# State-space stage of a decoder: products, scores and counts put in other places of the turns

## The chip, the cores and the metric

The kernel runs on one core of one Trainium2 chip. The metric is the device time of one execution in microseconds; of a kernel that was run several times, the median is given. A core has five engines with a queue of instructions each: TensorE (PE in the profile; PEld is its loading of weights), VectorE (DVE), ScalarE (ACT), GpSimd (POOL) and SyncE (SP, here the queue that issues transfers). Engines wait for one another by semaphores; within its queue each takes the instructions in order.

## The reference

The whole is a decoder of two layers on 2048 tokens of width 256 (16 blocks of 128). Each of its parts is `x = layernorm(x + part(x))`. The change touches one of them alone, the state-space part of the second layer, with a small memory behind it:

```python
xn = rmsnorm(x); zxbcdt = xn @ in_proj_w              # z 512, xBC 768, dt 8
xBC = silu(conv_b + four taps along the tokens of xBC)  # 128 tokens in a sequence
y = ssd(xs * dt, dt * A, B, C) + xs * D               # 8 heads of 64, state 128, chunks of 64
y = rmsnorm(y * silu(z)) @ out_proj_w
scores = sigmoid(relu(y @ scorer_w1) @ scorer_w2)      # one for each token
summaries = y @ summ_w                                 # 64 wide
# a scan over all tokens keeps the 50 summaries of the highest scores over 0.5
q = y @ q_w; kk = pool @ k_w; vv = pool @ v_w
retrieved = softmax(q kk / 4, valid slots) @ vv
y = y + sigmoid([y, retrieved] @ gate_w) * retrieved   # if the scores' mean is over 0.3
return x + y
```

The kernel replaces the scan by ranks: for each token it counts how many scores are larger (or equal, and of an earlier token). A token with a rank under 50 and a score over 0.5 goes into that slot of the pool.

## The kernel before

Six stages follow one another; this one is `stage3`, which calls `ssm` (lines 1246 to 1768) and then `memory` (line 1771). Stage 4, cross attention, follows.

**Blocks, groups and turns.** A block is 128 tokens, a group four blocks (512 tokens). `squared`, `normed` and `turn` normalise and transpose the four groups ahead of the loop; group 0 is convolved there too. Then a loop of 18 turns runs (line 1683), n from 0 to 17. In `ssm` every engine takes its instructions in the order in which they are written; no planner reorders them there. (In `memory` only TensorE's order is as written, the other engines' is planned.) Turn n carries several blocks at once, each at another step:

- block n + 1: `decay` (line 1388, GpSimd, cs less csb into mT, two mT buffers), `inner` (1399: TensorE products of B and C, and transposes; VectorE reads them as bc and xd), `decayed` (1394, ScalarE twice), `joined` (1412, GpSimd, mT times bc)
- block n: `outer` (1441, TensorE, needs mT and xd), `skipped` (1451, VectorE, four instructions), `passed` (1459, GpSimd: yf times the gate sz)
- block n - 1: `measured` (1463, ScalarE squares yf into sq), `added` (1469, GpSimd, two adds that bring the four chunks of sq down to one), `projected` (1475, TensorE), `summed` (1481: one TensorE product with a column of ones, then ys on VectorE and the root yrs on GpSimd), `scaled` (1490: y on ScalarE, x on VectorE)
- block n - 2: `kept` (1496: TensorE transposes y, ScalarE copies it into yT)
- block n + 2: `spread` (a transfer of csb, on SyncE's queue; two csb buffers) and `gate`, `gate_tanh`, `gated` (1417 to 1439)
- two chunks of the next group's convolution: `convolved`, `taps`, `tanh`, `curved` (1290 to 1316), in turns with n % 4 < 3 and n < 11. So turns 3, 7 and 11 to 15 carry no convolution.

In turns with n % 4 < 3 `inner`, `decayed` and `joined` stand early in the turn, in the others behind `summed`. PSUM has 8 banks: four ps_m, two ps_o (projected sums, transposed y, summaries, key and value banks), one ps_y (outer, and every third key or value bank) and one ps_s, which `inner`, `summed`, scores and keys take one after the other.

**Scores and ranks.** Once a group's four blocks are in yT, `remembered(g)` (1503) makes in one go the hidden layer and the queries (TensorE L1507, VectorE, ScalarE), the summaries (L1515) and the scores (L1519, then ScalarE and VectorE). It runs at the end of turns 7, 11 and 13 and, for group 3, after the loop. `lined` and `ranked` (1529, 1537) spread the group's scores along a row and keep them as keys. `counted(g)` (1551) gives three functions: `equals` (VectorE, three instructions), `by_vector(b)` (VectorE, one or two instructions that compare the row with a key and sum up) and `by_scalar(b)` (the same with signs on ScalarE, and a small correction on GpSimd). The table `counts` (1678) says in which turn which block's counts are made; group 3's follow after the loop, half on each engine.

**Between them** `others(n)` (1605) works off key and value banks of stage 4: TensorE products, a ScalarE copy, a store on SyncE's queue. There are twelve.

**After the loop** `memory` runs twelve key and value parts of stage 4 on TensorE first (line 1791; two PSUM banks, each copied out by ScalarE, rows L1998, L2001, L2018 and L2022), while VectorE sums up ranks and makes the picks (L1795 to L1808); then TensorE gathers the pool (L1810), and so on.

Of the kernel before, what the change touches and what calls it, by code (L numbers as in the profile page):

```python
# [1245 lines left out]
def ssm(K, w, m, kv_banks):  # L1246
# [6 lines left out]
    with ExitStack() as ctx:  # L1253
# [16 lines left out]
        def normed(g):  # L1270
            rs = K.new(small, [P, 4], F32, "rs")
            K.rsqrt(small, rs, xn[g].ss, 1.0 / D, 1e-5, "rs_t")
            t = K.new(work, [P, SH, P], F32, "csb").rearrange("p (i h) t -> p i (h t)", i=4)
            xn[g].x = [t[:, i, :] for i in range(4)]
            for i in range(4):
                nc.vector.tensor_scalar(xn[g].x[i], x[4 * g + i], rs[:, i:i + 1], None, ALU.mult)
# [181 lines left out]

        def passed(n):
            s, at = st[n], slice(n % 2 * P, n % 2 * P + P)  # L1460
            nc.gpsimd.tensor_tensor(s.yf, s.yf, sz[n // 2][:, :, at], ALU.mult)
# [19 lines left out]
        def summed(n):  # L1481
            s = st[n]
            pn = K.new(ps, [P, 1], F32, "ps_s", bufs=1)
            nc.tensor.matmul(pn, s.sq[:, 0, :], K.ones[:, :1], start=True, stop=True)
# [18 lines left out]
        def remembered(g):  # L1503
# [4 lines left out]
            hid = K.new(work, [P, 512], F32, "acc", bufs=3)  # L1508
# [7 lines left out]
            nc.vector.tensor_copy(m.summ[:, 4 * g:4 * g + 4, :], psu)  # L1516
            psc = K.new(ps, [P, 4], F32, "ps_s", bufs=1)
# [133 lines left out]
        for n in range(2):  # L1651
# [27 lines left out]
            11: ((equals0, None), (vector0, 0, 1, 2, 3)), 13: ((equals1, None), (vector1, 4, 5), (scalar1, 0, 1)),  # L1679
            14: ((vector1, 6, 7), (scalar1, 2, 3)), 15: ((equals2, None), (vector2, 8, 9), (scalar2, 0, 1, 2, 3)),  # L1680
            16: ((vector2, 10, 11), (scalar2, 4, 5, 6, 7)),
        }
        for n in range(NB + 2):
# [10 lines left out]
            if old:  # L1694
                measured(n - 1)
                added(n - 1)
# [9 lines left out]
            if new and i < 3:  # L1706
                inner(n + 1)
            if late is not None:
                curved(*late)
            if new and i < 3:  # L1710
                decayed(n + 1)
                joined(n + 1)
            if n in (8, 12, 14):
                lined({8: 0, 12: 1, 14: 2}[n])
# [13 lines left out]
            if new and i == 3:  # L1728
# [3 lines left out]
            if n in (12, 14, 15):  # L1732
                others(1)
            if n == NB:
                others(2)
# [6 lines left out]
            if 1 < n <= NB + 1:  # L1742
# [8 lines left out]
            if n in (7, 11, 13):  # L1751
                remembered({7: 0, 11: 1, 13: 2}[n])
# [5 lines left out]
            if n in (8, 12, 14):  # L1758
                ranked({8: 0, 12: 1, 14: 2}[n])
        remembered(3)  # L1760
        lined(3)
        ranked(3)
        equals, by_vector, by_scalar = counted(3)
        equals(None)
        for k in range(8):
            by_scalar((0, 1, 2, 3, 4, 5, 14, 15)[k])
            by_vector((6, 7, 8, 9, 10, 11, 12, 13)[k])
# [855 lines left out]
```

## Time and profile before

| | us |
|---|---|
| median of 3 runs | 1404.76 (1403.98 to 1405.64) |
| the profiled execution, its own time | 1408.86 |
| its span, first to last instruction | 1407.2 |
| mean granted TensorE clock | 0.954 |
| busy in the span: PE, DVE, ACT, POOL | 1234.8, 824.7, 676.4, 495.5 |
| loop of turns and the scores after it (first square at 415.3, last keys at 656.2) | 240.9 |

Busy time is a mean over stages with different limits: TensorE is 88% busy over the whole, but in this stage it is not what the others wait for. A timeline row reads: start, length, engine, line of the kernel, operation, what it writes and reads with shapes, how many instructions are merged in the row, and in brackets how long the engine sat idle before and what ended that. TensorE's fp32 products show as two records each. Three rows of turn 7 as samples: the sum over sq behind the halving adds, then the gate product of block 7 and the decay of block 9 behind it on GpSimd.

```profile
530.92 0.38 PE L1484 MATMUL ps_s<-ones,sq 128*128 128x1 f32 x2 [1.41 <-POOL sq L1472]
```

```profile
535.32 1.26 POOL L1461 TENSOR_TENSOR yf<-yf,sz 128x512 f32<-128x512 f32 x1 [0.45 <-DVE yf L1455]
536.54 1.90 POOL L1390 TENSOR_TENSOR mT<-cs,csb 128x1024 f32<-128x1024 f32 x1
```

### The profile page before, as it was taken

The numbers are of one execution on the slowest core, as the hardware profiler recorded it, in microseconds if no ns is written. First come the engines' busy times: TensorE is split into PE (matmuls) and PEld (weight loads), VectorE is DVE, ScalarE is ACT, GpSimd is POOL, SyncE is SP. The second block draws the span as 40 slices with busy tenths as digits, with TensorE's granted clock in tenths as the row PEclk, the third lists the DMA queues.
The fourth block names the chain that finished last, engine by engine and source line by source line (L and its number), as shares of the span: only waits on it lengthen the run. The fifth ranks groups of instructions, "written<-read, shape, count | busy, mean of one in ns | idle before, by whom it ended". The sixth has DMA issues, their size and how long they took to land.

```text
span 1407.2 us, 19229 instructions
## 1 busy us (share of the span) xinstructions
PE 1234.8 (88%) x6731; PEld 843.2 (60%) x6743; DVE 824.7 (59%) x1755; ACT 676.4 (48%) x1733; POOL 495.5 (35%) x669
## 2 busy tenths in 40 slices
PE   4678887889978899866998999999889999999995
PEld 1455444666654566643655788877777655666553
DVE  7799968989957887856244565667333111211115
ACT  5779865778956665544223566654522111111110
POOL 4256547668861776640043233222202000000003
PEclk9899989989999999987899999999999999999998
DMA  8358324110011211100100222211005222232002
GB/s 311 131 174 295 114 79 85 17 39 31 32 50 60 74 51 46 53 16 24 52 0 1 73 78 62 75 61 45 1 8 187 71 98 68 78 105 96 17 8 75
DMA packets 63120, 103.53 MB, mean 74 GB/s; under 512 B 11920, under 2 KB 41712, under 8 KB 62768
## 3 DMA queue, kind: packets, MB, share of 16 engines
q1 hardware_dynamic: 60848, 96.76, 20.6%
q0 software_dynamic: 2176, 5.55, 1.9%
q8 instruction: 53, 0.87, 0.3%
q14 instruction: 43, 0.35, 0.1%
HBM read 81.74 MB, written 16.35 MB: 70 GB/s over the span
## 4 chain that ended last, share of the span: by engine, by line
PE 52%; DVE 29%; ACT 8%; POOL 6%; issue 4%; DMA 1%; another core or an unknown queue 0%; SPq 0%; DVEq 0%; ACTq 0%; POOLq 0%
PE ps_y L2453 7%; PE ps_m L2442 7%; PE ps_g L2442 7%; PE ps_m L1998 4%; DVE acc L1306 2%; PE ps_m L2129 2%; ACT s L2100 2%; PE ps_t L2120 2%; PE ps_m L2018 2%; DVE cT L1315 1%; DVE s L915 1%; DVE m L2094 1%; DVE s L2090 1%; PE ps_t L2109 1%; PE ps_s L2087 1%
## 5 line engine op out<-in xcount | busy, mean ns | idle before, releaser
L82 POOL TENSOR_SCALAR ln_t<-ln_mv 128x1 f32<-128x1 f32 (+1 forms) x84 | 16.6, 197 | 450.7 <-DVE ln_mv L90 309.1
L2447 DVE TENSOR_TENSOR h<-h,ps_m 128x512 f32<-128x512 f32 x60 | 41.3, 688 | 228.3 <-PE ps_m L2442 228.3
L2100 ACT ACTIVATE s<-s,m 128x128 f32<-128x128 f32 x256 | 99.4, 390 | 69.1 <-DVE m L2094 69.1
L2446 ACT ACTIVATE h<-ps_g 128x512 f32<-128x512 f32 x60 | 35.8, 597 | 171.0 <-PE ps_g L2442 171.0
L2442 PE MATMUL ps_g<-xin,w 128*128 128x512 f32 x224 | 106.3, 592 | 0.0
L2442 PE MATMUL ps_m<-xin,w 128*128 128x512 f32 x224 | 105.3, 592 | 0.0
L2453 PE MATMUL ps_y<-w,h 128*128 128x256 f32 x448 | 97.8, 379 | 0.0
L2453 PEld LDWEIGHTS ps_y<-w,h 128*128 128x128 f32 x448 | 85.1, 190 | 14.6 <-issue 3.3
L2104 POOL TENSOR_TENSOR s<-s,t 128x1024 f32<-128x1024 f32 x32 | 60.7, 1898 | 90.7 <-DVE t L2103 90.7
L927 ACT ACTIVATE s<-s,m 128x128 f32<-128x128 f32 x256 | 83.3, 395 | 11.7 <-DVE m L922 11.7
L2442 PEld LDWEIGHTS ps_m<-xin,w 128*128 128x128 f32 x224 | 42.5, 190 | 51.4 <-issue 50.2
L2442 PEld LDWEIGHTS ps_g<-xin,w 128*128 128x128 f32 x224 | 42.0, 190 | 46.4 <-issue 45.0
L1998 PE MATMUL ps_m<-xT,half 128*128 128x256 f32 x256 | 62.6, 389 | 2.6 <-DVE qT L2003 1.9
L2454 ACT COPY y<-ps_y 128x256 f32<-128x256 f32 x30 | 11.2, 372 | 104.7 <-PE ps_y L2453 67.7
L2090 DVE TENSOR_TENSOR s<-ps_s,hide 128x1024 f32<-128x1024 f32 x32 | 39.2, 1224 | 35.9 <-PE ps_s L2087 35.9
L2129 PE MATMUL ps_m<-half,oT 128*128 128x256 f32 x256 | 59.3, 385 | 0.0
L1306 DVE SCALAR_TENSOR_TENSOR acc<-ps_m,l1a_conv_w,acc 128x508 f32<-128x508 f32 (+2 forms) x72 | 53.3, 740 | 3.5 <-ACT acc L1299 1.8
L1998 PEld LDWEIGHTS ps_m<-xT,half 128*128 128x128 f32 x256 | 47.4, 194 | 9.2 <-DVE qT L2003 2.3
L2129 PEld LDWEIGHTS ps_m<-half,oT 128*128 128x128 f32 x256 | 47.4, 190 | 7.5
L83 POOL TENSOR_TENSOR ln_rs<-ln_t,mhalf 128x1 f32<-128x1 f32 (+1 forms) x84 | 48.7, 579 | 7.0
L2100 ACT ACTIVATION_READ_ACCUMULATOR s<-s,m 128x1 f32 x256 | 48.2, 188 | 0.0
L1414 POOL TENSOR_TENSOR mT<-mT,bc 128x1024 f32<-128x1024 f32 x16 | 37.8, 2360 | 28.4 <-ACT mT L1396 16.3
(524 smaller groups left out, 3102.1 us busy)
## 6 DMA issues: line engine op xcount, KB each, us to landing
w<-in_w_gate_dram SPq DMA_DIRECT2D x9, 1024.0 KB
csb<-cs_dram SPq DMA_DIRECT2D x16, 512.0 KB
w<-in_l1f_gateT_dram SPq DMA_DIRECT2D x14, 512.0 KB
w<-in_l1f_upT_dram SPq DMA_DIRECT2D x14, 512.0 KB
w<-in_l1f_downT_dram SPq DMA_DIRECT2D x14, 512.0 KB
k<-kv SPq DMA_DIRECT2D x20, 256.0 KB
v<-kv SPq DMA_DIRECT2D x20, 256.0 KB
ring<-k SPq DMA_DIRECT2D x10, 512.0 KB
```

Of the source, the lines that this page charges most:

```text
L83: return self.nc.gpsimd.tensor_tensor(out, t, self.mhalf[: out.shape[0], :n], ALU.pow)
L927: nc.scalar.activation(at, at, AF.Exp, bias=m[h][:, i:i + 1])
L1306: nc.vector.scalar_tensor_tensor(accv[:, :, j:], pcv[:, :, :P - j], w.conv[:, c, TAPS - 1 - j:TAPS - j], accv[:, :, j:], ALU.mult, ALU.add,)
L1414: nc.gpsimd.tensor_tensor(st[n].mT, st[n].mT, bc, ALU.mult)
L1998: nc.tensor.matmul(pq[:, j, :], wt[k][:, at], src[:, k, :], start=(k == 0), stop=(k == KD - 1))
L2090: nc.vector.tensor_tensor(half(b, j), pss.rearrange("p r c k -> p (r c) k"), hide.unsqueeze(1).to_broadcast([P, 8, P]), ALU.add,)
L2100: nc.scalar.activation(at, at, AF.Exp, bias=m[j][:, i:i + 1], accum_out=t[j][:, i:i + 1])
L2104: nc.gpsimd.tensor_tensor(half(b, j), half(b, j), t[j].unsqueeze(2).to_broadcast([P, 8, P]), ALU.mult)
L2129: nc.tensor.matmul(py[b], oT[b][:, c, :], w.o[c // 4][:, c % 4, :], start=(c == 0), stop=(c == NC - 1))
L2442: nc.tensor.matmul(ps[:, j, :], m[k][:, c * P:(c + 1) * P], self.r.xin[:, k, e, cols], start=(k == 0), stop=(k == KD - 1),)
L2447: nc.vector.tensor_tensor(h, h, pu, ALU.mult)
L2453: nc.tensor.matmul(pd, rows(c), w.down[c // 4][:, c % 4, :], start=(c == 0), stop=(c == FI // P - 1))
```

## The change

`full(n)` names the turns with convolution, n < 11 and n % 4 < 3. In the other turns the gate product `passed` goes to VectorE, `added` falls away (`summed` multiplies all four chunks of sq with the ones and sums in PSUM instead), and `inner`, `decayed`, `joined` stand behind `summed` in turns 12 to 14 too. `remembered` is cut in two: `hidden_scores`, ahead of `outer`, with hidden layer, queries and summaries, and `scored`, at the end of the turn, with the scores. Group 2 has both in turn 14 instead of 13, and its row and keys in turn 15 instead of 14. The counts are spread over turns 11 to 17 in another way; VectorE's counts of group 2 (blocks 8 to 11) move behind the loop, and there all counts of group 3 are VectorE's. `others` moves from turns 12, 14, 15 and twice 16 to 12, 13, 15, 16 and 17; in turn 16 `kept` comes ahead of it. Ahead of the loop, half of the products of `normed` go to GpSimd for groups 2 and 3.

```diff
@@ -1273,7 +1273,8 @@
             t = K.new(work, [P, SH, P], F32, "csb").rearrange("p (i h) t -> p i (h t)", i=4)
             xn[g].x = [t[:, i, :] for i in range(4)]
             for i in range(4):
-                nc.vector.tensor_scalar(xn[g].x[i], x[4 * g + i], rs[:, i:i + 1], None, ALU.mult)
+                on = nc.gpsimd if g > 1 and i > 1 else nc.vector
+                on.tensor_scalar(xn[g].x[i], x[4 * g + i], rs[:, i:i + 1], None, ALU.mult)

         def turn(g):
             xnT[g] = K.new(grp, [P, KD, 512], F32, "xnT", bufs=4)
@@ -1456,9 +1457,13 @@
                     s.yf[:, c, :], cT[n // 4][:, c, mine(n)], w.d[:, c:c + 1], s.py[:, c, :], ALU.mult, ALU.add,
                 )

+
+        def full(n):
+            return n < 11 and n % 4 < 3
+
         def passed(n):
             s, at = st[n], slice(n % 2 * P, n % 2 * P + P)
-            nc.gpsimd.tensor_tensor(s.yf, s.yf, sz[n // 2][:, :, at], ALU.mult)
+            (nc.gpsimd if full(n) else nc.vector).tensor_tensor(s.yf, s.yf, sz[n // 2][:, :, at], ALU.mult)

         def measured(n):
             s = st[n]
@@ -1481,7 +1486,9 @@
         def summed(n):
             s = st[n]
             pn = K.new(ps, [P, 1], F32, "ps_s", bufs=1)
-            nc.tensor.matmul(pn, s.sq[:, 0, :], K.ones[:, :1], start=True, stop=True)
+            chunks = 1 if full(n + 1) else DI // P
+            for c in range(chunks):
+                nc.tensor.matmul(pn, s.sq[:, c, :], K.ones[:, :1], start=(c == 0), stop=(c == chunks - 1))
             t = K.new(small, [P, 1], F32, "ys")
             nc.vector.tensor_scalar(t, pn, 0.25 / DI, 1e-5, ALU.mult, ALU.add)
             s.yrs = K.new(small, [P, 1], F32, "yrs")
@@ -1500,12 +1507,12 @@
             nc.scalar.copy(m.yT[:, :, n * P:(n + 1) * P], pt)


-        def remembered(g):
+        def hidden_scores(g):
             cols = slice(512 * g, 512 * g + 512)
             pq = K.new(ps, [P, 512], F32, "ps_m", bufs=4)
             for k in range(KD):
                 nc.tensor.matmul(pq, w.qw1[:, k, :], m.yT[:, k, cols], start=(k == 0), stop=(k == KD - 1))
-            hid = K.new(work, [P, 512], F32, "acc", bufs=3)
+            hid = held["hid"] = K.new(work, [P, 512], F32, "acc", bufs=3)
             nc.vector.tensor_scalar(hid[SUM:, :], pq[SUM:, :], 0.0, None, ALU.max)
             nc.scalar.copy(m.qT[:, cols], pq[:SUM, :])
             psu = K.new(ps, [P, 4, SUM], F32, "ps_o")
@@ -1514,6 +1521,9 @@
                 for k in range(KD):
                     nc.tensor.matmul(psu[:, i, :], m.yT[:, k, at], w.summ[:, k, :], start=(k == 0), stop=(k == KD - 1))
             nc.vector.tensor_copy(m.summ[:, 4 * g:4 * g + 4, :], psu)
+
+        def scored(g):
+            hid = held["hid"]
             psc = K.new(ps, [P, 4], F32, "ps_s", bufs=1)
             for i in range(4):
                 nc.tensor.matmul(
@@ -1676,9 +1686,9 @@
         order, late = (4, 5, 0, 1, 2, 3), None
         (equals0, vector0, _), (equals1, vector1, scalar1), (equals2, vector2, scalar2) = (counted(g) for g in range(3))
         counts = {
-            11: ((equals0, None), (vector0, 0, 1, 2, 3)), 13: ((equals1, None), (vector1, 4, 5), (scalar1, 0, 1)),
-            14: ((vector1, 6, 7), (scalar1, 2, 3)), 15: ((equals2, None), (vector2, 8, 9), (scalar2, 0, 1, 2, 3)),
-            16: ((vector2, 10, 11), (scalar2, 4, 5, 6, 7)),
+            11: ((equals0, None), (vector0, 0, 1)), 12: ((vector0, 2, 3),),
+            13: ((equals1, None), (vector1, 4), (scalar1, 0, 1)), 14: ((vector1, 5), (scalar1, 2, 3)),
+            15: ((vector1, 6, 7),), 16: ((equals2, None), (scalar2, 0, 1, 2, 3)), 17: ((scalar2, 4, 5, 6, 7),),
         }
         for n in range(NB + 2):
             g, i = divmod(n, 4)
@@ -1693,7 +1703,8 @@
                 gate_tanh()
             if old:
                 measured(n - 1)
-                added(n - 1)
+                if full(n):
+                    added(n - 1)
             if late is not None:
                 tanh(*late)
             if ahead:
@@ -1703,15 +1714,15 @@
                     gated()
                 gate(n + 2)
                 gate_tanh()
-            if new and i < 3:
+            if new and full(n):
                 inner(n + 1)
             if late is not None:
                 curved(*late)
-            if new and i < 3:
+            if new and full(n):
                 decayed(n + 1)
                 joined(n + 1)
-            if n in (8, 12, 14):
-                lined({8: 0, 12: 1, 14: 2}[n])
+            if n in (8, 12, 15):
+                lined({8: 0, 12: 1, 15: 2}[n])
             if ahead:
                 taps(*c[0])
                 tanh(*c[0])
@@ -1725,21 +1736,27 @@
                 curved(*c[0])
             if old:
                 summed(n - 1)
-            if new and i == 3:
+            if new and not full(n):
                 inner(n + 1)
                 decayed(n + 1)
                 joined(n + 1)
-            if n in (12, 14, 15):
+            if n in (7, 11, 14):
+                hidden_scores({7: 0, 11: 1, 14: 2}[n])
+            if n in (12, 13, 15):
                 others(1)
             if n == NB:
-                others(2)
+                kept(n - 2)
+                others(1)
             if now:
                 outer(n)
                 skipped(n)
                 passed(n)
             if old:
                 scaled(n - 1)
-            if 1 < n <= NB + 1:
+            if 1 < n < NB:
+                kept(n - 2)
+            if n > NB:
+                others(1)
                 kept(n - 2)
             if ahead:
                 taps(*c[1])
@@ -1748,23 +1765,26 @@
                     gate(n + 2)
             else:
                 late = None
-            if n in (7, 11, 13):
-                remembered({7: 0, 11: 1, 13: 2}[n])
+            if n in (7, 11, 14):
+                scored({7: 0, 11: 1, 14: 2}[n])
             if n == 13:
                 held["junk"] = K.new(work, [P, SH, P], F32, "csb").rearrange("p h t -> p (h t)").bitcast(BF16)
             for what, *which in counts.get(n, ()):
                 for b in which:
                     what(b)
-            if n in (8, 12, 14):
-                ranked({8: 0, 12: 1, 14: 2}[n])
-        remembered(3)
+            if n in (8, 12, 15):
+                ranked({8: 0, 12: 1, 15: 2}[n])
+        hidden_scores(3)
+        vector2(8)
+        scored(3)
         lined(3)
         ranked(3)
-        equals, by_vector, by_scalar = counted(3)
+        for b in (9, 10, 11):
+            vector2(b)
+        equals, by_vector, _ = counted(3)
         equals(None)
-        for k in range(8):
-            by_scalar((0, 1, 2, 3, 4, 5, 14, 15)[k])
-            by_vector((6, 7, 8, 9, 10, 11, 12, 13)[k])
+        for b in range(NB):
+            by_vector(b)
         assert next(banks, None) is None and not gates


```

## The prediction

> **What bounds the kernel now.** I read the page, the chain of waits, the table of stretches, and each engine's timeline through the state-space stage and the stage that picks its memory. The stage runs from 415 to 656 us in turns, one token block each. Up to turn 10 a turn with convolution takes 10.3 us, set by VectorE and GpSimd in turns; from turn 11 no engine is full, and the chain hops between them. Two stretches, turns 15 to 17 and what follows:
>
> ```profile
> 623.00:646.00 23.00, 14.08 (x50) 6.57 (x48) 13.28 (x31) 10.65 (x26) 8.34 (x23) 0.84 0.09 34
> ...
> 656.00:689.00 33.00, 27.54 (x112) 20.09 (x112) 14.64 (x35) 16.61 (x33) 0.00 (x0) 0.85 0.20 64
> ```
>
> Columns: stretch, length, busy TensorE, weight loads, VectorE, ScalarE, GpSimd, granted clock, DMA. In 23 us no engine is busy for more than 14.1: this stretch is made of waits. ScalarE's rows show two, and the end:
>
> ```profile
> 641.39 0.48 ACT L1493 ACTIVATE y<-ps_o,yrs 128x256 f32<-128x256 f32 x1
> ...
> 645.55 0.35 ACT L1500 COPY yT<-ps_o 128x256 f32<-128x256 f32 x1
> ...
> 665.93 1.07 ACT L2001 COPY ring<-ps_m 128x512 f32<-128x512 f32 x2
> ```
>
> The last block's scaled output y waits to 641.39 behind two key/value copies, and its transposed copy yT to 645.55 behind four sign counts (642.29 to 645.55). The final group's sign counts hold the ring copies to 665.93, and so TensorE:
>
> ```profile
> 645.96 3.39 PE L1507 MATMUL ps_m<-yT,l1a_qw 128*128 128x512 f32 x4 [3.07 <-ACT yT L1500]
> ...
> 656.20 5.11 PE L1998 MATMUL ps_m<-ctxT,l1x_W_k 128*128 128x256 f32 x16 [0.46 <-DVE above L1548]
> ...
> 666.57 6.74 PE L1998 MATMUL ps_m<-ctxT,l1x_W_k 128*128 128x256 f32 x16 [5.25 <-ACT ring L2001]
> ...
> 687.02 2.07 PE L1810 MATMUL ps_s<-pick,summ 128*64 128x50 f32 x32
> ```
>
> VectorE has the picks ready at 671.0, 16 us before TensorE, which first works off twelve key/value parts of 1.72 each, comes to them:
>
> ```profile
> 656.18 0.69 DVE L1560 TENSOR_TENSOR junk<-row,key 128x512 bf16<-128x512 f32 x1
> ...
> 666.16 1.94 DVE L1573 TENSOR_SCALAR_CACHE_REDUCE junk<-row,key 128x1664 bf16<-128x1664 f32 x1
> ...
> 668.02 0.17 DVE L1790 TENSOR_SCALAR valid<-score 128x16 f32<-128x16 f32 x1
> ...
> 669.99 1.05 DVE L1808 TENSOR_TENSOR pick<-pick,valid 128x400 f32<-128x400 f32 x2
> ...
> 689.12 0.20 DVE L1817 COPY poolT<-ps_s 64x50 f32<-64x50 f32 x1 [18.07 <-PE ps_s L1810]
> ```
>
> One more reading prices what moves to VectorE: an operation with two SBUF inputs beside a long GpSimd one.
>
> ```profile
> 483.27 2.37 POOL L1414 TENSOR_TENSOR mT<-mT,bc 128x1024 f32<-128x1024 f32 x1 [1.58 <-ACT mT L1396]
> ```
>
> ```profile
> 484.28 1.90 DVE L1315 SCALAR_TENSOR_TENSOR cT<-cT,acc 128x512 f32<-128x512 f32 x1
> ```
>
> Alone it takes 0.68; here it ends 0.54 after GpSimd's does. So it waits for the running GpSimd instruction and then gets in: I add 0.55 to that end each time.
>
> **The change part by part**, in the clock of this execution (span 1407.2, time 1408.86, 4.1 above the median of 1404.76; I take the difference over to the median).
>
> *Normalising groups 2 and 3.* Two of four products go to GpSimd: 2 x 0.47 (row L1614, same shape) against 2 x 0.28 on VectorE. Side by side this saves 0.5, one after the other it adds up to 0.6; TensorE's transposes follow anyway. Taken: +0.2.
>
> *Turn 3.* The halving adds (0.69 + 0.80 on GpSimd) go; three more one-column products take 0.75 (four of 64 rows take 0.98, one 0.28), and VectorE's list, not the sum, now sets ys, 0.2 earlier. The gate product (GpSimd 1.27, from 496.01 behind the join) goes to VectorE: the join ends at 495.85, + 0.55 = 496.4 against 497.28. ScalarE's square, the next convolution's copy and its taps start 0.85 earlier; the turn's last combination, behind the next join, 0.95. Taken: -0.95; -1.3 if the product meets no join, +1.0 if it must also let the following decay (1.90) pass.
>
> *Turn 7.* Before, TensorE does products, summaries and scores of group 0 in one go (534.49 to 539.86) before turn 8's convolution. Now the first two come ahead of outer. Without the adds ys comes at 531.0 (531.5), block 8's products end at 531.9, hidden and summaries (1.72 + 1.73) at 535.35, outer 536.3, transposes 536.65 (kept takes the ps_o bank that frees first, the summaries' one), scores 537.6: the convolution starts 2.25 earlier. VectorE's product waits for decay(9) (outer frees its buffer at 536.3; 1.90) to 538.75, still 2 ahead of the copy that needs it. Taken: -2.3; -0.6 if hidden and outer run at half clock as before (2.56 for 1.72, 1.60 for 1.02).
>
> *Turns 11 to 17*, walked through with the rows' durations (outer 1.02, skip 1.05, product 0.65, x 0.4, a key/value bank 1.72 + copy 0.6, products for the next block 0.8, equals 2.15):
> - 11: ys 574.6, products 575.45, hidden and summaries 578.9, outer 579.9. decay(13) holds GpSimd to 581.8, so the gate product ends at 582.35. x, scores, equals0, two counts (0.79 + 0.92): 587.05.
> - 12: line, sz, ys 588.5; products (now behind the sum) 589.3, bank 591.0, outer 592.0; decay(14) to 593.9, product 594.45; x, two counts (0.93 + 0.89), keys: 597.15. Before, the turn's keys ended at 594.84.
> - 13: ys 597.85, products 598.65, bank 600.35, outer 601.4; decay(15) to 603.3, product 603.85; x, equals1, one count (1.46): 607.9. Before, with group 2's products in it, the two counts ended at 615.4.
> - 14: ys 608.0, products 608.85, hidden and summaries 612.3, outer 613.3, scores 614.6; VectorE (no decay left to wait for) 615.9, one count 617.3.
> - 15: bank 619.8, its copy (outer needs that bank) 620.45, outer 621.55, product 623.35, x, two counts 2.8, keys 627.0.
> - 16: the sum waits for the key copy, since both use the one ps_s bank: 627.65. ys, yrs 628.4; bank 629.7, copy 630.35, y 630.8, four sign counts of 0.84: 634.15.
> - 17: copy 0.6, yT 0.35: 635.1.
>
> So hidden_scores(3) starts at 635.15, not 645.96: -10.8. Some 8 us of that is only put off: counts 8 to 11 of group 2. The sync queue holds the same twelve stores; spread(15) still follows block 12's store (592.04, its transfer over by 597), ahead of decay(15) at 601.4. For half clock in more places than before I add 1.0, up to 5.8 (below). Taken: -9.8.
>
> *The end*, from the start S of that product. Summaries are out at S + 5.6 as before; vector2(8) (0.67 + 1.32) now stands ahead of the scores' VectorE steps, with line, keys and all ranks behind it: the keys are done at S + 11.45, not S + 10.2. Then counts 9 to 11 (5.95), equals 2.18, twelve counts of 0.785 (9.4), four double ones of 2.52 (10.0), and 2.5 to the first half of the picks: S + 41.5. Before, TensorE reached the picks at S + 41.06, so +0.4. Its own work is no cover any more: without sign counts the ring copies follow at once and the twelve parts end some 22.3 after the keys, at S + 33.8; it then idles 7.7 us. The row at 666.57, after a gap of 5.25, takes 6.74 for what takes 3.45 warm, so the picks and the part behind them cost 3.3 more; taken 3.0, with 0 to 3.6 as bounds. End: +3.4.
>
> [...]
>
> Sum: 0.2 - 0.95 - 2.3 - 9.8 + 3.4 = -9.4 us: 1397.8 of span, **1395.4** for the median.
>
> **The rivals.**
> - *Half clock in turns 12 to 16.* I put gaps of up to 2.6 us between TensorE's bursts there. For it: in 533 to 537 the clock was 0.60 after gaps of 1.4 and 0.25, in 630 to 634 0.72 after one of 2.26. Against: after 2.66 and 3.00 us (588.8, 615.75) the bank took its full-clock 1.96. Two turns at half clock cost 2 x (0.65 + 1.72 + 1.02) = 6.8, of which 1.0 is in the sum: about 1401. [...]
> - *Slower: the ring copies stay behind the counts.* The ring tiles lie where stage 3's work tiles lay; the first of them was written at 665.93, just as the last sign count ended, and the queued loads of the next weights waited for that tile too. I read it as ScalarE's order. If instead they wait for the stage's last count, that is now VectorE's, at S + 39: then the picks end 23.1 later, as from 665.93 to 689.02, at S + 62.1 instead of S + 43.06, +19.0. With -9.8 for turns 11 to 17 and -3.05 for the steps before them, this gives +6.1: 1411. The sign turns where the first copy starts later than S + 32.8 (there + 23.1 eats the 12.85 gained before S).
> - *No effect:* the early turns gain nothing, turns 11 to 17 only the counts put off (-8.0), the end takes 3.4, and one turn at half clock 3.4: -1.2, 1403.6.
> - *More:* turns 11 to 17 keep -10.8 and the end costs 0.4, or every term takes its low end: 1390 to 1391.3.
>
> **How the numbers follow.** Forecast 0.60 (1391.3 to 1400 on its own), half clock 0.18, slower 0.14, about nothing 0.04, more 0.04. A measurement tells 0.2%, 2.8 us, from no change. Faster 0.60 + 0.18 + 0.04 = 0.82, same 0.04, slower 0.14. The bounds of the terms give -14.7 to 0; with the second case and part of the fourth, the range is 1389.5 to 1405.5.
>
> **What would show it.** hidden_scores(3) near 633 (early gains included); group 2's hidden product in turn 14 without a wait on yT; the first ring copy some 3 us after the last keys; a TensorE gap of 7 to 8 us before the picks, ended by VectorE, and a half clock behind it; VectorE's product ending 0.55 after a decay in turns 7 and 11 to 13. Wrong if GpSimd keeps the product waiting through two instructions, if ring copies start after VectorE's last count, or if ScalarE's order delays yT past 640.

## The result, and the profile after

The changed kernel takes **1400.83 us** (median of 20 runs, 1394.09 to 1410.53), the kernel before, run beside it, 1404.99 (20 runs, 1400.49 to 1410.79): a ratio of 0.9966, with a 95% interval of 0.9951 to 0.998. That is 2.8 to 6.9 us faster, 4.2 by the medians, where 9.4 were forecast. Two later comparisons gave 0.9943 (0.9919 to 0.9967) and 0.9971 (0.9955 to 0.9988).

The profiled execution of the changed kernel took 1398.93 us, with a span of 1397.1. Its timeline rows at the places that the prediction names follow: first TensorE's, then ScalarE's first ring copy (a finished key and value part copied out of PSUM) and VectorE's last step of the picks. TensorE's rows L1514 are the hidden products, L1830 is the gather of the pool, called the picks below:

```profile
603.66 1.88 PE L1514 MATMUL ps_m<-yT,l1a_qw 128*128 128x512 f32 x4
...
630.85 2.63 PE L1514 MATMUL ps_m<-yT,l1a_qw 128*128 128x512 f32 x4 [2.15 <-ACT yT L1507]
...
673.04 3.62 PE L1830 MATMUL ps_s<-pick,summ 128*64 128x50 f32 x32 [6.13 <-issue]
...
681.19 5.15 PE L1871 MATMUL ps_m<-kkT,qT 64*128 64x50 f32 x32
...
646.78 0.58 ACT L2021 COPY ring<-ps_m 128x512 f32<-128x512 f32 x1 [3.91 <-PE ps_m L2018]
...
672.37 1.05 DVE L1828 TENSOR_TENSOR pick<-pick,valid 128x400 f32<-128x400 f32 x2
```

Group 2's hidden product no longer waits for yT. The last one starts at 630.85 instead of 645.96, the ring copies come 4 us after the keys instead of behind all counts, and TensorE runs dry for 6.1 us before the picks, which then take 3.62 instead of 2.07. The two stretches shown before, at their new place (columns as there: stretch, length, busy TensorE, weight loads, VectorE, ScalarE, GpSimd, granted clock, DMA):

```profile
608.00:631.00 23.00, 16.27 (x87) 10.35 (x84) 12.43 (x36) 11.17 (x28) 2.48 (x10) 1.00 0.07 24
641.00:674.00 33.00, 26.41 (x93) 18.86 (x92) 30.12 (x68) 7.61 (x13) 0.00 (x0) 0.81 0.19 64
```

Behind the keys VectorE is now busy for 30.1 of 33 us (14.6 before): it sets the end, as worked out.

Up to that product this execution is within 1 us of what was predicted, and still the median is not. To see why, single executions have to be compared place by place, because they differ where the code is the same: the stage's first root on GpSimd (**R**) came between 413.6 and 421.4 in the traces of this study, and from the first gate addition of the memory on VectorE (**F**, L1890, now L1910) to the last instruction it took 693.4 to 700.2. Below, **S** is the start of the last hidden product.

### The profile page after: what moved, and what is told of

The parts are those of the page before. It is cut to its first block, busy times and chain, and to the rows that moved or that the text cites. A ratio compares the mean times of both kernels' runs of the same rounds, so it can differ in the third digit from the quotient of the medians.

```text
span 1397.1 us, 19300 instructions
## 1 busy us (share of the span) xinstructions
PE 1231.7 (88%) x6779; PEld 849.2 (61%) x6791; DVE 834.5 (60%) x1778; ACT 666.8 (48%) x1713; POOL 477.8 (34%) x642
## 3 DMA queue, kind: packets, MB, share of 16 engines
q1 hardware_dynamic: 60848, 96.76, 20.8%
## 4 chain that ended last, share of the span: by engine, by line
PE 52%; DVE 29%; ACT 7%; POOL 5%; issue 4%; DMA 2%; another core or an unknown queue 0%; SPq 0%; DVEq 0%; POOLq 0%; ACTq 0%
PE ps_y L2473 7%; PE ps_m L2462 7%; PE ps_g L2462 7%; PE ps_m L2018 4%; DVE acc L1307 3%; ACT s L2120 2%; PE ps_t L2140 2%; PE ps_m L2149 2%; PE ps_m L2038 2%; DVE cT L1316 2%; DVE s L915 1%; DVE m L2114 1%; DVE s L2110 1%; PE ps_t L2129 1%; PE ps_s L2107 1%
## 5 line engine op out<-in xcount | busy, mean ns | idle before, releaser
L2473 PE MATMUL ps_y<-w,h 128*128 128x256 f32 x448 | 97.8, 379 | 0.0
L2473 PEld LDWEIGHTS ps_y<-w,h 128*128 128x128 f32 x448 | 85.1, 190 | 14.6 <-issue 3.3
L2124 POOL TENSOR_TENSOR s<-s,t 128x1024 f32<-128x1024 f32 x32 | 60.7, 1896 | 91.1 <-DVE t L2123 91.1
L2110 DVE TENSOR_TENSOR s<-ps_s,hide 128x1024 f32<-128x1024 f32 x32 | 39.2, 1224 | 35.9 <-PE ps_s L2107 35.9
L2149 PE MATMUL ps_m<-half,oT 128*128 128x256 f32 x256 | 59.3, 385 | 0.0
L1298 PE MATMUL ps_m<-xnT,l1a_in_proj 128*128 128x512 f32 x96 | 46.8, 611 | 0.4 <-ACT y L1268 0.4
```

The lines of the kernel that those rows point to most:

```text
L1298: nc.tensor.matmul(pc, w.inp[:, k, at:at + P], xnT[g][:, k, :], start=(k == 0), stop=(k == KD - 1))
L2110: nc.vector.tensor_tensor(half(b, j), pss.rearrange("p r c k -> p (r c) k"), hide.unsqueeze(1).to_broadcast([P, 8, P]), ALU.add,)
L2124: nc.gpsimd.tensor_tensor(half(b, j), half(b, j), t[j].unsqueeze(2).to_broadcast([P, 8, P]), ALU.mult)
L2149: nc.tensor.matmul(py[b], oT[b][:, c, :], w.o[c // 4][:, c % 4, :], start=(c == 0), stop=(c == NC - 1))
L2473: nc.tensor.matmul(pd, rows(c), w.down[c // 4][:, c % 4, :], start=(c == 0), stop=(c == FI // P - 1))
```

## Experiments

**The same two kernels again** (`before_again`, `after_again`, and `after_third` later), no edit.

> The kernel before, unchanged: a second trace of it. First profile: S - R = 228.6, F - S = 58.8, last instruction - F = 702.5. The change is worth -11.9 up to S, +5.8 from S to F and about -0.7 behind by the first pair of traces; if the pairs agree to 1 us this stands, and the rest of what the spans differ by (3.2 ahead of the stage, where the code is the same) is scatter between executions.

> The changed kernel once more, unchanged: a second execution with its trace. S is the start of hidden_scores(3)'s product, F the first gate product behind the pool (VectorE), R the stage's first root. First profile: S - R = 216.65, F - S = 64.5, last instruction - F = 701.7. If these come back within 1 us, the trace differences can be read to that; if F - S moves by several us while VectorE's picks stay at S + 41 to 42, the half clock behind TensorE's gap differs from execution to execution.

> The changed kernel once more, beside the next three. S - R was 216.65 and 225.28 in its two traces, and 219.59, 217.48 and 219.61 in three kernels with the same code up to there; theory: once more between 216 and 226, with half clock in turn 12 (R + 167) or 14 (R + 187) where it is over 218, each stretch some 3.4 us or a multiple long, and F - S 65 to 67. Median 1400 to 1402.

The F of the first two texts, and of the two kernels that follow, is TensorE's first gate product, always 2.64 us ahead of VectorE's F; from here on all values are VectorE's.

| us | R to S | S to F | the turns 11 to 17: block 7's root to S |
|---|---|---|---|
| before, two traces | 228.6, 229.0 | 61.35, 61.36 | 98.1, 98.1 |
| after, first trace | 216.65 | 67.2 | 88.5 |
| after_again (median 1400.95) | 225.3 | 65.3 | 97.8 |
| after_third (median 1402.36) | 225.2 | 62.2 | 97.8 |

The kernel before repeats to 0.5 us. The changed one does not: the 12 us gained ahead of S shrink to 3.5 in two executions of three, all of it in turns 11 to 17. Its timeline rows in turns 12 and 14, first of the first execution, then of the second:

```profile
582.75 0.49 PE L1403 MATMUL ps_s<-cT 128*128 128x128 f32 x2 [2.56 <-DVE ys L1493]
...
583.51 1.88 PE L1972 MATMUL ps_o<-l1x_W_v,ctxT 128*128 128x512 f32 x4
...
599.02 1.97 PE L1484 MATMUL ps_o<-l1a_out_proj,yf 128*128 128x256 f32 x8 [2.37 <-DVE yf L1466]
...
603.66 1.88 PE L1514 MATMUL ps_m<-yT,l1a_qw 128*128 128x512 f32 x4
```

```profile
587.49 0.80 PE L1403 MATMUL ps_s<-cT 128*128 128x128 f32 x2 [2.56 <-DVE ys L1493]
...
588.93 3.62 PE L1972 MATMUL ps_o<-l1x_W_v,ctxT 128*128 128x512 f32 x4
...
606.74 3.21 PE L1484 MATMUL ps_o<-l1a_out_proj,yf 128*128 128x256 f32 x8 [2.37 <-DVE yf L1466]
...
613.14 3.62 PE L1514 MATMUL ps_m<-yT,l1a_qw 128*128 128x512 f32 x4
```

The gaps are the same to the hundredth, 2.56 and 2.37 us, ended by the same releasers. Behind them the same products take 1.88 in one execution and 3.62 in the other: the granted clock is at half. The same seven and eleven microseconds after R in the table of stretches (R + 167 to 174, R + 187 to 198), first execution, then second:

```profile
581.20:588.20 7.00, 5.45 (x35) 3.52 (x36) 4.18 (x12) 1.85 (x4) 4.55 (x3) 1.00 0.19 63
...
601.20:612.20 11.00, 9.18 (x68) 7.45 (x67) 7.49 (x23) 4.49 (x11) 3.27 (x4) 1.00 0.00 1
```

```profile
586.65:593.65 7.00, 6.16 (x22) 3.63 (x24) 1.77 (x5) 0.96 (x2) 2.89 (x2) 0.51 0.00 0
...
606.65:617.65 11.00, 10.65 (x32) 7.95 (x33) 5.58 (x12) 3.04 (x5) 3.27 (x4) 0.53 0.01 1
```

The two executions differ in where the granted clock steps. Read in short stretches, a step of the clock can be placed to a few hundredths of a microsecond. In the first execution the steps between 600 and 700 us stand at 632.05, 649.12, 669.59, 679.83, 683.25 and 690.08: 17.07, 20.47, 10.24, 3.42 and 6.83 apart, that is 5, 6, 3, 1 and 2 times 3.41. In the traces of before, after_again, after_third, kept_warm2 and best2 the steps read lie whole multiples of 3.41 us apart as well (in before, between 600 and 640, at 601.04, 607.86, 631.76 and 638.58: 6.82, 23.90 and 6.82), and in best3 and more_parts one stretch of half clock lasted 3.4. So in these traces the steps lie on one grid of 3.41 us, and what differed is how that grid lay to the work. Two intervals of it at turn 14's gap, first execution (counted back from the step at 632.05, 11 intervals after the first one begins), then second:

```profile
594.50:597.91 3.41, 2.15 (x20) 1.05 (x18) 1.54 (x5) 2.15 (x6) 3.31 (x4) 1.00 0.22 79
597.91:601.32 3.41, 2.29 (x14) 2.12 (x14) 3.34 (x5) 3.08 (x6) 0.42 (x1) 1.00 0.02 5
```

```profile
603.89:607.30 3.41, 1.04 (x8) 0.74 (x6) 3.22 (x7) 2.65 (x8) 2.04 (x2) 1.00 0.22 79
607.31:610.72 3.41, 3.41 (x13) 2.88 (x11) 3.08 (x7) 2.26 (x3) 0.00 (x0) 0.50 0.02 5
```

In the first a boundary cuts the gap of 2.37 us into 1.26 and 1.11, and the clock stays; in the second the whole gap lies in one interval, and the clock falls at that interval's end, at 607.31. In after_third and more_parts the whole gap lies in one interval too, and the clock falls (at 608.95 and 605.96); in best3 a boundary cuts it into 1.51 and 0.86, and the clock stays at 1.00. Three more traces have the gap, and show by times what came of it. From block 12's root on GpSimd to block 14's it took 20.8 us in the first execution and in best3, where the clock stayed, and 24.7, 24.7 and 21.6 in after_again, after_third and more_parts, where it fell. It took 20.8 in counts_back and 21.6 in signs_back; kept_warm has its half clock in a row shown below. So half clock followed the gap in five of eight.

At turn 12's gap of 2.56 us the clock fell in after_again, after_third and best3 (at 586.84, 588.47 and 585.66), with 1.91, 1.93 and 2.56 us of it in the interval ahead of the fall; it stayed in the first execution, where 0.66 lay ahead of the boundary and 1.90 behind it. From block 11's root to the decay behind it, it took 3.72 there and 6.70, 6.72 and 5.38 in those three; with 6.68, 6.53 and 5.34 in more_parts, signs_back and counts_back, that is half clock in six of seven. The idle time in one interval did not decide alone: the gap of 3.00 us before 615.75 in the kernel before put 1.94 us into one, and no half clock followed (1.00 from 607.86 to 631.76).

**More parts ahead of the gather.**

```diff
-        meanwhile(12)
+        meanwhile(15)
```

> The changed kernel with fifteen instead of twelve key and value parts of stage 4 ahead of the pool's gather. Theory (VectorE's list of counts sets when the picks are ready, TensorE runs dry before them, and then works at half clock): three parts of 1.72 fill 5.2 of the 6.1 us gap, the picks' end stays at S + 45 to 46 less 1.6 for full clock, the part behind and the gate's products run at full clock (1.7 and about 1.5 less), so F - S falls from 64.5 by 4 to 6; three parts fewer behind the memory give back up to 5.2 more if TensorE is the bound there. Total -5 to -10 against the changed kernel. Rival (the gap is VectorE's list alone and the clock costs nothing): F - S within 1 of 64.5, total -5 at most from the parts behind. Rival (a third ring bank's copies or stores delay it): F - S grows.

Measured: 1399.46 (ratio 0.9927, 0.9901 to 0.9953), beside 0.9943 for the changed kernel in the same comparison: no gain that can be told. The gap is filled, and the picks run at full clock, but the clock falls behind them all the same (L1871 takes 5.67; the same product takes 3.73 at full clock, in the kernel before and in best2):

```profile
678.01 2.04 PE L1830 MATMUL ps_s<-pick,summ 128*64 128x50 f32 x32 [1.15 <-issue]
...
682.98 5.67 PE L1871 MATMUL ps_m<-kkT,qT 64*128 64x50 f32 x32
```

From the picks' end to F it takes 21.45 us, as in the changed kernel (21.4) and not as before (18.2). F is at S + 63.5. So the list of counts holds (the picks start at S + 40 whether TensorE waits for them or not); that the half clock behind them comes from the gap does not. R to S was 219.6 here, with half clock in turns 12 and 14 again, in the second of them for 3.4 us:

```profile
605.00:606.00 1.00, 0.59 (x3) 0.57 (x4) 1.00 (x3) 0.71 (x3) 0.00 (x0) 0.98 0.00 0
606.00:609.00 3.00, 3.00 (x11) 2.44 (x9) 2.90 (x6) 2.23 (x3) 0.00 (x0) 0.50 0.02 5
609.00:610.00 1.00, 0.82 (x6) 0.74 (x5) 0.29 (x3) 0.00 (x0) 0.00 (x0) 0.81 0.00 0
```

A mean of 0.98 is half clock for 0.04 us of that microsecond, one of 0.81 for 0.38: 0.04 + 3 + 0.38 = 3.4 us.

**Counts 8 to 11 back ahead of the keys**, into VectorE's idle time: 8 ahead of `scaled` in turn 16, 9 and 10 in turn 17, 11 behind the last hidden layer.

```diff
-        def hidden_scores(g):
+        def hidden_scores(g, between=None):
...
+            if between is not None:
+                vector2(between)
...
-            15: ((vector1, 6, 7),), 16: ((equals2, None), (scalar2, 0, 1, 2, 3)), 17: ((scalar2, 4, 5, 6, 7),),
+            15: ((vector1, 6, 7),), 16: ((equals2, None), (scalar2, 0, 1, 2, 3)), 17: ((vector2, 9, 10), (scalar2, 4, 5, 6, 7)),
...
+            if n == NB:
+                vector2(8)
...
-        hidden_scores(3)
-        vector2(8)
+        hidden_scores(3, 11)
...
-        for b in (9, 10, 11):
-            vector2(b)
```

> The changed kernel with VectorE's counts 8 to 11 of group 2 taken back into idle stretches of VectorE ahead of the last keys: 9 and 10 at the end of turn 17's list, 8 in turn 16, 11 behind hidden_scores(3)'s first step. None behind the loop. Theory: S later by at most 0.7, the keys done at about S + 11.2, VectorE's list behind them 5.95 shorter, so the picks are ready at S + 35.5 and TensorE comes to them from its parts with a gap below 1 us, at full clock: the picks end at S + 37 to 38 instead of S + 45.8, F - S falls from 64.5 to about 54, total -9 to -11 against the changed kernel, about 1390. Rival (the put-off counts are not what the end waits for): F - S within 2 of 64.5. Rival (the clock does not matter, only the list does): F - S falls by 6 and no more.

Measured: **1390.21** (0.9864, 0.983 to 0.9898), 10.7 below the changed kernel beside it. In the trace:

```profile
666.97 2.04 PE L1831 MATMUL ps_s<-pick,summ 128*64 128x50 f32 x32 [1.60 <-issue]
...
671.95 5.65 PE L1872 MATMUL ps_m<-kkT,qT 64*128 64x50 f32 x32
```

The picks start at S + 35.9 and F is at S + 59.35: 5.6 less than the mean of the changed kernel's three (64.9). That is the size that the rival "only the list matters" named: counts 9 to 11, which stood behind the keys, are 5.95 of list. That the clock does not matter is not shown, since the half clock behind the picks stays here. Where the rest of the 10.7 comes from stays open: in this trace it lies ahead of S (R to S 217.5), where the code is the same up to turn 16 and this execution was spared most of the half clock.

**The last group's counts divided as before**, and, the other way round, **the kernel before with all of them on VectorE**. In the first the ring copies stand behind ScalarE's sign counts again; the second makes the same edit to the kernel before, the other way round.

```diff
-        for b in range(NB):
-            by_vector(b)
+        for k in range(8):
+            by_scalar((0, 1, 2, 3, 4, 5, 14, 15)[k])
+            by_vector((6, 7, 8, 9, 10, 11, 12, 13)[k])
```

> The changed kernel with the last group's counts divided as before: eight on VectorE, eight by signs on ScalarE; counts 9 to 11 of group 2 stay behind the loop. Theory: the sign counts hold the ring copies again, so TensorE comes to the picks late, at about S + 42.3, when VectorE (ready at about S + 32) has long been done: no gap ahead of the picks, full clock behind, VectorE's first gate addition F at S + 62.6 instead of S + 65.3 to 67.2; 3 to 4 faster than the changed kernel, about 1397.5. Rival (VectorE alone is the better division here as well): F - S at or over 66, no gain.

> The kernel before with one part of the change alone: all counts of the last group on VectorE. Theory: the ring copies start 3 us after the keys, the twelve parts end near S + 33.5, VectorE's picks are ready near S + 34.3, so the picks start at S + 34 to 36 instead of S + 41; behind them TensorE works at half clock as in the kernel with the counts taken back (21.4 from the picks' end to F instead of 18.2). F - S falls from 61.4 to 56 to 59.5: 2 to 5 faster than before. Rival (the ring copies wait for the stage's last count on whichever engine): F - S over 70, slower by 10 or more.

Measured: 1397.83 (0.9942, 0.9923 to 0.9961) and 1399.15 (0.9948, 0.9927 to 0.9968), beside 1406.26 for the kernel before. Rows of the first kernel, then of the second:

```profile
676.91 2.07 PE L1831 MATMUL ps_s<-pick,summ 128*64 128x50 f32 x32
...
656.11 1.07 ACT L2022 COPY ring<-ps_m 128x512 f32<-128x512 f32 x2
...
666.09 1.05 DVE L1829 TENSOR_TENSOR pick<-pick,valid 128x400 f32<-128x400 f32 x2
```

```profile
679.67 2.04 PE L1809 MATMUL ps_s<-pick,summ 128*64 128x50 f32 x32 [1.65 <-issue]
...
659.14 0.58 ACT L2000 COPY ring<-ps_m 128x512 f32<-128x512 f32 x1 [3.71 <-PE ps_m L1997]
```

With the counts divided, VectorE has the picks ready at S + 30.6 and TensorE comes to them at S + 40.4 without a gap: F at S + 60.7, against 62.2, 65.3 and 67.2. So with counts 9 to 11 waiting behind the loop, VectorE alone looks like the worse division, by one trace against three; the times do not tell (0.9942 here, 0.9943 to 0.9971 for the changed kernel in other comparisons). In the kernel before, where none wait, it is the better one: ring copies at S + 14.2, picks at S + 34.7, F at S + 58.2 instead of 61.4. That one edit alone gives 7.1 us by the medians, as much as the whole change; 3.2 of it shows between S and F. In the trace the rest lies behind F (694.1 instead of 699.8), within what that stretch scatters, so its cause is not shown.

**TensorE kept busy in the gaps.** Products that nobody reads, two of 128x512 (1.7 us), in the gap of turn 12 and, at first, in turn 13.

```diff
+        def warm(k):
+            pj = K.new(ps, [P, 512], F32, "ps_m", bufs=4)
+            for _ in range(k):
+                nc.tensor.matmul(pj, K.ones, xnT[3][:, 0, :], start=True, stop=True)
...
+            if n == 13:
+                warm(2)
             if old:
                 projected(n - 1)
...
                 summed(n - 1)
+            if n in (12, 13):
+                warm(2)
             if new and not full(n):
                 inner(n + 1)
```

> The changed kernel with idle TensorE time filled in three places by products that nobody reads (two of 128x512 each, 1.7 us): in turns 12 and 13 between the sum over sq and inner, and in turn 13 ahead of projected. The output stays the reference's. In two traces of the unchanged kernel TensorE idles 2.4 to 2.6 us there; in one the clock stays 1.00 and S - R is 216.65, in the other it is 0.50 for 6.4 us and for 10.7 us and S - R is 225.28; two kernels with the same code up to there give 219.59 and 217.48. Theory (gaps of that length let the clock fall in some executions and not in others): clock 1.00 from R + 165 to R + 200, S - R 216 to 217.5, the median 2 to 4 below the changed kernel's 1401, with few runs over 1403. Rival (the clock does not hang on those gaps): S - R between 216 and 225 as before, no gain in the median. Rival (the products are in the way): up to 5 slower.

A miss: 1405.18, ratio 0.9996 (0.9976 to 1.0016), where the changed kernel had 0.9943 to 0.9971 in its own comparisons; the two were not run side by side. The gap that ends at R + 187 is turn 14's, not turn 13's. In turn 13 the products stood in front of work that was ready, and the gap that they were meant for was still there, with half clock behind it (the last row; 1.97 at full clock):

```profile
591.37 1.88 PE L1471 MATMUL ps_m<-xnT,ones 128*128 128x512 f32 x4
593.09 1.89 PE L1489 MATMUL ps_o<-l1a_out_proj,yf 128*128 128x256 f32 x8
...
603.73 2.54 PE L1489 MATMUL ps_o<-l1a_out_proj,yf 128*128 128x256 f32 x8 [2.37 <-DVE yf L1466]
```

In turn 12 they held the clock at 1.00, as in all four kernels that have them there; without them it fell in six traces of seven. Mended:

```diff
-            if n == 13:
+            if n == 14:
                 warm(2)
             if old:
                 projected(n - 1)
...
-            if n in (12, 13):
+            if n == 12:
                 warm(2)
```

> The products that nobody reads, put right: two of 128x512 (1.7 us) in turn 12 between the sum over sq and inner (the gap at R + 165.3, where they held the clock at 1.00 in the two kernels that had them), and two in turn 14 ahead of projected (the gap of 2.4 us at R + 184.5; the run before had them in turn 13, where TensorE had no gap, so they only delayed it). Theory: clock 1.00 from R + 165 to R + 200, S - R 216 to 217.5, the median 2 to 4 below the changed kernel of this call. Rival (the clock falls all the same, or the products delay what follows): S - R 219 or more, no gain.

Measured: 1399.93 (0.9955, 0.9936 to 0.9973), 2.4 below the changed kernel beside it, and R to S 217.1 against that one's 225.2. The same two stretches as above:

```profile
584.19:591.19 7.00, 6.34 (x39) 4.30 (x40) 4.18 (x10) 1.97 (x5) 4.80 (x3) 1.00 0.25 83
...
604.19:615.19 11.00, 9.50 (x69) 7.86 (x70) 7.24 (x22) 3.84 (x10) 3.27 (x4) 1.00 0.00 1
```

Of the eight microseconds gained in these two traces 6.7 are given back by F: the clock now falls at S, for some 17 us (it was read at half from 635.41 to 649.19; an end near 652.5 is an estimate from the row of ring products behind, 10.09 us where 7.07 is full clock), the keys come at S + 12.2 instead of S + 9.9, and F at S + 68.9 instead of S + 62.2. From R to F it is 286.0 against 287.4. The intervals of the two ratios overlap, so the times do not show the 2.4. The granted clock shows that the products held it in these two turns, not that the kernel is faster for it.

**A kernel that beats both.** Counts 8 to 11 taken back, all of `normed` on VectorE, and then the unread products of turns 12 and 14 with two more ahead of the last hidden product (`best2`). An earlier attempt (`best1`) had the misplaced products of `kept_warm` and thirteen parts ahead of the gather. `best3` is the first of these two edits alone, on the kernel with the counts taken back:

```diff
-                on = nc.gpsimd if g > 1 and i > 1 else nc.vector
-                on.tensor_scalar(xn[g].x[i], x[4 * g + i], rs[:, i:i + 1], None, ALU.mult)
+                nc.vector.tensor_scalar(xn[g].x[i], x[4 * g + i], rs[:, i:i + 1], None, ALU.mult)
...
+        warm(2)
         hidden_scores(3, 11)
```

> The kernel with the counts taken back (1390.2) and three more edits: the idle TensorE time of turns 12 and 13 filled as in the run that keeps the clock, thirteen key and value parts ahead of the gather instead of twelve, and all of normed's products on VectorE. Theory: S - R 216 to 217 (normed 0.4 less); the thirteenth part fills the 1.6 us gap ahead of the picks, so that the clock stays full behind them and F - S falls from 59.35 to 56 to 57.5; median 1384 to 1388. Rival (the half clock behind the picks does not come from the gap ahead of them): F - S 59 to 60, median 1388 to 1390.

> The kernel with the counts taken back, and all of normed's products on VectorE again. Theory: 0.4 to 0.6 less than the kernel with the counts taken back alone: first decay 0.6 earlier after R, median 1389 to 1391. Rival (GpSimd's half of normed is worth something): first decay later, 1391 or more.

> The kernel before this one, with the filled gaps of turns 12 and 14 and two more unread products ahead of the last hidden product (TensorE waits 2.16 us for yT there, and the clock falls behind it in five of seven traces). Theory: S - R 216 to 217, the keys done at S + 9.9 instead of S + 11.7, F - S about 57.5; median 1385 to 1388, 3 to 4 below the kernel without the products. Rival (the unread products cost as much as the clock that they keep): within 1.5 of it, or slower.

| | median, us | ratio to before (95%) | R to S | S to F |
|---|---|---|---|---|
| best1 | 1392.14 | 0.9891 (0.987 to 0.9912) | 220.2 | 59.4 |
| best3 | 1388.31 | 0.987 (0.9849 to 0.9892) | 216.9 | 59.3 |
| best2 | **1384.03** | 0.9845 (0.9824 to 0.9865) | 216.9 | 53.9 |

best1 answers its question: the thirteenth part closes the gap ahead of the picks, and the clock falls behind them as before (rows of best1). In best2 it stays up through both products:

```profile
676.22 2.07 PE L1839 MATMUL ps_s<-pick,summ 128*64 128x50 f32 x32
...
681.23 5.69 PE L1880 MATMUL ps_m<-kkT,qT 64*128 64x50 f32 x32
```

```profile
665.48 2.04 PE L1840 MATMUL ps_s<-pick,summ 128*64 128x50 f32 x32 [0.25 <-issue]
...
670.45 3.73 PE L1881 MATMUL ps_m<-kkT,qT 64*128 64x50 f32 x32
```

best2 is 22 us faster than the kernel before, and its five runs lie within 4.6 us (1382.2 to 1386.78), those of the changed kernel beside it within 9.3. Of its 5.4 us between S and F against best3, 2.2 are the keys (S + 9.6 instead of S + 11.8), the rest the clock behind the picks. The intervals of best3 and best2 overlap too, though only one of best2's five runs is slower than best3's fastest. In turn 14 the products were not enough in best2: the clock fell there for 3.4 us (R + 188), as it had not in kept_warm2.

## Why the prediction was right or wrong

The sign was right and the time lay in the range; the size was not, -4.2 instead of -9.4. Step by step, in traces:

| step | forecast | measured |
|---|---|---|
| normed (first decay after R) | +0.2 (-0.5 to +0.6) | +0.6 to +0.8: 33.7, 32.9 and 32.9 in three traces, against 33.05 and 32.2 in two of before and 32.1 in best3 |
| turn 3 | -0.95 | -1.0 in the first pair (from first decay to block 3's root: 54.0 to 53.0); 55.3 in the second trace of before, 53.0 in the others of after |
| turn 7 (block 3's root to block 7's) | -2.3 | -1.9 in all traces (43.4 to 41.4) |
| turns 11 to 17 | -9.8 | -9.6, -0.3, -0.3 |
| the end (S to F) | +3.4 | +5.8, +4.0, +0.8 |

**normed** cost its upper bound or a little more: GpSimd's two products took 2.00 together, not 0.94, beside VectorE's two, which took 0.84, not 0.56.

```profile
421.78 2.00 POOL L1277 TENSOR_SCALAR csb<-x,rs 128x256 f32<-128x256 f32 x2
```

**Turns 3 and 7** went as worked out from one pair of rows: VectorE's two-input product, started beside a GpSimd instruction, ends a little after that instruction does. In turn 12 it starts at 587.62, takes 1.38 and ends 0.54 after the decay that runs from 586.56; in turns 3, 7, 11 and 13 of the first trace it ends 0.54 to 0.56 after the join or the decay. In turns 14 and 15, with no GpSimd instruction beside it, it takes 0.69:

```profile
587.62 1.38 DVE L1466 TENSOR_TENSOR yf<-yf,sz 128x512 f32<-128x512 f32 x1
...
586.56 1.90 POOL L1391 TENSOR_TENSOR mT<-cs,csb 128x1024 f32<-128x1024 f32 x1 [0.49 <-POOL mT L1415]
```

**Turns 11 to 17 are the step that failed**, and in it the one term "for half clock in more places than before I add 1.0, up to 5.8": it was mis-sized. The walk through the turns gave -10.8, and -9.6 came in the execution that kept its clock there, 1.2 short. In the others half clock, in turns 12 and 14 above all, took another 9.3; over the three traces, and three kernels with the same code up to turn 15 (-5.9, -8.0, -6.0), the step was worth -5.0 in the mean. In place of the 1.0 stand 5.8, the term's upper bound, the 1.2 of the walk included. With the other forecasts left as they are the sum would have been 0.2 - 0.95 - 2.3 - 5.0 + 3.4 = -4.65, against -4.2 measured. The three traces of the changed kernel say the same: R to F is 6.3 shorter, 0.4 longer and 2.8 shorter than before, 2.9 shorter in the mean, and of the 6.5 that this lacks of the forecast 6.4 lie in turns 11 to 17. They are three executions of 42, so the shares of the median are an estimate. Nor is the end independent of the turns: where the turns kept their clock (the first trace, kept_warm2), it fell right behind S for 17.1 and some 17 us, and S to F was longest, 67.2 and 68.9.

So the rival "half clock in turns 12 to 16", put at 1401 and given 0.18, is the one that came: 1400.83. What spoke against it in the profile of before, two rows that ran at full clock after 2.66 and 3.00 us of idling, was true of that execution only; both gaps were cut by a boundary of the grid, into 1.24 and 1.42 and into 1.94 and 1.06. A gap of 2.4 to 2.6 us kept the clock in one execution and lost it in the next. The half clock of 0.60 after 1.4 us, which I had noted, should have weighed as much. One of the prediction's sums is slightly off, without weight for this: the low bounds of the terms add up to -14.5, not -14.7.

**The end.** The gap (6.1 to 7.4 us, forecast 7.7), its cause (VectorE's list) and the half clock behind it came as written. The price went three ways: in the first execution 1.1 for the later start of the picks (S + 42.2 against 41.06), 1.55 for the picks at half clock and 3.1 behind them, 5.8 in all; in the third the picks start at S + 40.0, because the keys come 2.2 earlier when the clock is full from S on (it comes back at 646.49, 0.2 behind S), and the clock falls behind them for 3.4 us only (697.69 to 701.11): +0.8 is left. The half clock cost 4.7, 5.1 and 1.9 in the three traces, where 3.0 was taken with 3.6 as the upper bound, and the later start of the picks 1.1, -1.1 and -1.1, where 0.4 was taken; that the two made up 3.5 in the mean, against 3.4, is luck in part. The reason was half right: with the gap filled the picks run at full clock, but the clock still falls behind them (more_parts, best1). Why it falls there stays open. In the kernel before it falls 9.6 us after the start of picks that run at full clock (687.02, the step at 696.61), with TensorE shown as busy for 9.60 us of the 9.60 from 687.00 on, in best2 9.2 us after (665.48, 674.68); in counts_back, more_parts, last_alone and best1 it falls during the product that starts 5.0 us after such picks (5.65 to 5.76 instead of 3.73).

**The slower rival**, ring copies behind the stage's last count, is refuted: the first ring copy came at S + 15.9 (13.7 in the later traces), with 24 us of VectorE's counts still to go. It was ScalarE's order. last_alone shows it in the kernel before as well.

**What the change gave away** was not foreseen as a choice: it puts all of the last group's counts on VectorE (worth 3.2 between S and F by itself) and in front of them 5.95 us of put-off counts. VectorE had idle time for these ahead of the keys; with them there, S to F is 5.6 shorter.

## What to carry to other kernels

Work that is put off is only gone if the engine that does it later is not the one that the next stage waits for; look for idle time of that engine ahead of the hand-over first. A walk through the rows gave the chain of seven turns to 1.2 us, but the TensorE gaps in it did not act the same in each execution: the one of 2.56 us was followed by half clock in six traces of seven, the one of 2.37 in five of eight, and two of 2.66 and 3.00 in the kernel before were not. Price such a gap as a chance of half clock, not by what it did in one profile: get a second trace, or fill the gap. Products that nobody reads can pay only where TensorE is certain to be idle; one turn off, they delayed the work behind them (1405.18 with them in turn 13, 1399.93 in turn 14). And the clock that was held in one place fell in the next: of the 8 us gained ahead of S in kept_warm2's trace 6.7 were lost behind it.

## What the runs showed of the hardware

Half-clock stretches behind the gaps of turns 12 and 14 lasted, worked out as above from the granted clock of single microseconds, 3.4, 6.8 or 10.2 us: in after_again 6.8 and 10.2, in after_third the same, in best3 3.4 in turn 12, in more_parts 3.4 in turn 14. Steps of 3.4, then, on the grid shown above. Where the gap of 2.37 us lay on the grid went with the outcome in the five traces read there: whole in one interval, and the clock fell in three of three; cut into parts of 1.51 at most, and it stayed in two of two. TensorE was busy for 10.65 of the 11 us around the stretch of 10.2 in after_again, and for 15.02 of the 17.07 us at half clock behind S in the first trace. What sets the grid, and how long the clock stays at half, no run here shows.
